# A cross-attention block on one Trainium2 core: where the attention weights are turned, and the order of pairs 3 to 5 and of the end

## The chip, the cores and the metric

The kernel runs on 1 core of one Trainium2 chip. The metric is the device time in microseconds (us). Five engines work side by side, each through its own instructions in their written order: TensorE (PE in the profile: matmuls; PEld: the weight loads that go with them), VectorE (DVE), ScalarE (ACT), GpSimd (POOL) and SyncE (SP, which here only issues DMAs). ACT's queue issues DMAs too.

## The reference

All tensors are float32. There are 128 sequences of 128 tokens with 256 features, `x` for the queries and `ctx_1024` for keys and values; 16 heads of 16 features.

```python
q = (query @ Wq + bq).reshape(b, s, 16, 16).transpose(0, 2, 1, 3)      # k and v likewise, from ctx
scores = einsum('bhqd,bhkd->bhqk', q, k) / sqrt(16)
scores = where(j < i, scores, -1e30)                                     # strictly earlier keys alone
attn = softmax(scores); attn[:, :, 0, :] = 0
ctx = einsum('bhqk,bhkd->bhqd', attn, v)
x = layer_norm(query + ctx @ Wo + bo, ln1_g, ln1_b)
out = layer_norm(x + relu(x @ W1 + b1) @ W2 + b2, ln2_g, ln2_b)         # W1: 256x1024, W2: 1024x256
```

## The kernel before, in words

**Tiling.** Two sequences make a pair; there are 64 pairs, p = 0 to 63, and 256 tokens in each. Scores have queries in partitions: the upper half of the queries (`hi` = 1, against all 128 keys) and the lower half (`hi` = 0, against the first 64 keys) are apart, since the mask leaves out later keys. The upper half has 2048 elements in a partition and is worked in two parts (`ONE`, heads 0 to 7, and `TWO`, heads 8 to 15), the lower half has 1024 (`ALL`).

**The stages of a pair**, with the lines that the profile names:
- `tokens` (L243, DVE) turns the loaded blocks of x or ctx into `xT`, `cT`; `load`, `load_tokens` and `load_ahead` (L92, L99) issue their DMAs on SP.
- `queries`, `keys` (L257, PE; L268 and L279, ACT) and `values` (L289, PE), with `values_out` (L299, L304 on ACT, and the DMA `vd<-vz`, L303, on ACT's queue).
- `scores` (L323) or `scores_both` (L357) on PE. `scores` makes one half, in PSUM banks 0 to 3. `scores_both` makes both: the upper half in banks 0 to 3, the lower half in banks 6, 7, 4 and 5.
- `mask` (L371, DVE) adds the mask and so empties the banks into `sm`; `maximum` (L382 on DVE, and on POOL the subtraction, L383); `exponential` (L390, ACT); `sums` (L402 and L403 on DVE, and on POOL the multiplication by the inverse of the sum, L404).
- `turn` (L417, DVE): a transposition of the weights in blocks of 32x32, into `tb`; three for a pair (upper `ONE`, upper `TWO`, lower). `bring` (L432): 16 DMAs, u = 0 to 15, that carry block row i = u // 4 and block column j = u % 4 of `tb` to its place in `pT`. `tb` and `pT` have one buffer each, so the `bring` of a pair starts after the `weigh` of the pair before.
- `weigh` (L464, L474, PE): weights times values, 96 short matmuls into bank 7. It reads blocks i = 0 and 1 (u = 0 to 7) for the first sequence of the pair (s = 0), then i = 2 and 3 (u = 8 to 15) for the second (s = 1). `context` (L486, ACT) copies the result to `cxT`.
- `attention_out` (L493, PE, bank 5), `attention_sum` (L519, DVE), `stats` (L506, L507, DVE), `deviation` and `shift` (L513, L514, L558, POOL), `norm1` (L535, ACT), `residual1` (L547, L550, POOL), `add_bo` (L250, POOL).
- `turn_x1`: a transposition `tbx` on DVE (L644), then `across`: four DMAs `x1t<-tbx` to DRAM (L235) and, when they have landed, one DMA `x1T<-x1t` back (L238).
- `hidden` (L680, PE; L686, ACT): x1 times W1 for eight chunks f, in four steps of two chunks that use banks 2, 3, 4 and 0, each followed by two ReLUs into `hT`. `second` (L698, PE, bank 6): eight matmuls in the program for each sequence s. The profile has twice as many matmuls as the program, here as everywhere, each with its weight load.
- `second_sum` (L706, DVE), `stats`, `scale_and_shift` (POOL), `norm2` (L572, ACT), `finish` (L578, L579, POOL), `store` (L587, the DMA `out_dram<-t` on ACT's queue).

**What sets the order.** `manual_schedule` keeps each engine's instructions in the order in which the program writes them; waits between engines are added by the framework from what reads and writes what. A bank that gets a new tile waits for the last reader of the old one. The start (pairs 0 and 1, before the functions below) and the functions `third` (L859, p = 2), `fourth` (L910, p = 3) and, for p = 4 to 63, `step(p)` (L937) write the order by hand; the lines after the loop (L1002 to L1078) empty the pipeline.

In `step(p)` PE has: `weigh(p-2)`, `scores_both(p)`, `queries(p+1)`, `attention_out(p-2)`, `keys(p+1)`, `values(p)`, `hidden(p-3)`, `second(p-3)`. DVE has the three `turn(p-1, ...)` between the masks and maxima of pair p. SP has: the loads of `load_ahead(p)`, then `bring(p-1)`, after the third turn, then the five DMAs of `turn_x1(p-2)`. In the last step and after the loop half of the weights, u = 8 to 15, are brought on ACT's queue.

In `fourth` the scores of pair 3 are made by `scores_both`, and `second(0)`, which writes bank 6, stands after them; the low scores of strip 0, in bank 6 too, are emptied by `mask(3, 0, A)`, the last masks of the pair.

Of the kernel before, what the change touches and what calls it, by code (L numbers as in the profile page):

```python
# [10 lines left out]
ALU = mybir.AluOpType  # L11
# [8 lines left out]
def tile_cross_attention_block(  # L20
# [205 lines left out]
                )  # L226
        return pt

    def across(dst, src, name):


        n = src.shape[2]
        mid = dram.tile([NS, NS, 32, n], F32, tag=name[: name.index("_")], name=name)
        for i in range(NS):
            nc.sync.dma_start(  # L235
                mid[i].rearrange("j b n -> b j n"), src[32 * i : 32 * i + 32]
            )
        nc.sync.dma_start(dst, mid.rearrange("i j b n -> (j b) i n"))  # L238

    def tokens(p, which):  # L240
        st = states.setdefault(p, {})
        st[which + "T"] = proj.tile([P, KC, TP], F32, tag=which + "T", name=f"{which}T_{p}")
        nc.vector.transpose(  # L243
            st[which + "T"], blocks_of.pop((which, p)).rearrange("p k u f -> p k (u f)")
        )
# [17 lines left out]
    def queries(p):  # L263
        st = states[p]
        st["qT"] = proj.tile([P, KC, TP], F32, tag="qT", name=f"qT_{p}")
        pq = project(wq, st["xT"], at_bank(4, f"pq_{p}") if p > 3 else bank(f"pq_{p}"))
        for m in range(KC):
            nc.scalar.activation(  # L268
                st["qT"][:, m, :], pq[:, m * TP : (m + 1) * TP], AF.Identity,
                bias=bqs_c[:, m : m + 1], scale=QSCALE,  # L270
            )
# [116 lines left out]
    def exponential(p, hi, part):  # L388
        sm = states[p]["sm", hi]
        nc.scalar.activation(sm[:, part, :], sm[:, part, :], AF.Exp)  # L390
# [229 lines left out]
    def scale_w1():  # L620
        for k in range(KC):
            nc.scalar.activation(
                w1[:, k, :], w1[:, k, :], AF.Identity, bias=0.0, scale=g1_c[:, k : k + 1]
            )
# [13 lines left out]

    def turn_x1(p):
        st = states[p]
        tb = ffn.tile([P, NS, 4 * 32], F32, tag="tbx", name=f"tbx_{p}")
        nc.vector.transpose(  # L644
            tb.rearrange("p j (u a) -> p u j a", a=32),
            st["x1"].rearrange("p s (k j a) -> p (s k) j a", k=KC, a=32),
        )
        x1T = ffn.tile([P, NS, 4 * 32], F32, tag="x1T", name=f"x1T_{p}")
        across(x1T, tb, f"x1t_{p}")
        st["x1T"] = x1T.rearrange("p i (s k a) -> p s i k a", s=2, k=KC)  # L650

    def turn_x1_on_pe(p):
# [37 lines left out]
            if between:  # L690
                between(f)

    def second(p, s, fs=range(FC)):
        st = states[p]
        if s == 0 and fs[0] == 0:
            st["py"] = at_bank(6, f"py_{p}")
        for f in fs:
            nc.tensor.matmul(  # L698
                st["py"][:, s * D : (s + 1) * D], st["hT"][:, f, s * P : (s + 1) * P],
                w2[:, f, :], start=(f == 0), stop=(f == FC - 1),  # L700
            )

    def second_sum(p):
        st = states[p]
# [137 lines left out]
    def load_ahead(p):  # L842
        if p % 2 == 0 and p + 4 < NP:
            load([p + 4, p + 5], "x")
        if p % 2 == 1:
            if p + 3 < NP:
                load([p + 3, p + 4], "c")
            if 3 < p < NP - 1:
                load_tokens((p + 1) // 2)
# [9 lines left out]
    def third():  # L859
# [47 lines left out]
        residual1(p - 1)  # L907
        hidden(0, range(3 * FC // 4, FC), lambda f: bring(p, nc.scalar, EVERY[8:]))

    def fourth():  # L910
        p = 3
        load_ahead(p)
        scores_both(p)
        mask(p, 0, B)
        mask(p, 1, A)
        maximum(p, 1, ONE)
        second(0, 0)
        exponential(p, 1, ONE)
        mask(p, 1, B)
        maximum(p, 1, TWO)  # L920
        second(0, 1)
        scale_w1()
        mask(p, 0, A)
        maximum(p, 0, ALL)
        queries(p + 1)
        exponential(p, 1, TWO)
        nc.gpsimd.tensor_tensor(b1e_c, b1e_c, b1_c, ALU.add)
        sums(p, 1, ONE)
        exponential(p, 0, ALL)
        tokens(p + 2, "x")  # L930
        keys(p + 1)
        second_sum(0)
        sums(p, 1, TWO)
        sums(p, 0, ALL)
        tokens(p + 2, "c")

    def step(p):  # L937
        last = p == NP - 1
        load_ahead(p)
        weigh(p - 2)  # L940
        context(p - 2)
        scores_both(p)
        if p > 4:
            second_sum(p - 4)
        turn(p - 1, 1, 0)
        if p > 4:
            residual1(p - 3)
            finish(p - 5)
            add_bo(p - 1)
        mask(p, 0, B)  # L950
        mask(p, 1, A)
        maximum(p, 1, ONE)
        turn(p - 1, 1, 1)
        if not last:
            queries(p + 1)
        if p > 4:
            store(p - 5)
        attention_out(p - 2)
        mask(p, 1, B)
        maximum(p, 1, TWO)  # L960
        exponential(p, 1, ONE)
        turn(p - 1, 0, 0)
        bring(p - 1, nc.sync, EVERY[: 8 if last else 16])
        mask(p, 0, A)
        maximum(p, 0, ALL)
        if not last:
            keys(p + 1)
        else:
            bring(p - 1, nc.scalar, EVERY[8:])
        exponential(p, 1, TWO)  # L970
        attention_sum(p - 2)
        values(p)
        stats(p - 4, states[p - 4]["t2"], 2)
        stats(p - 2, states[p - 2]["t1"], 1)
        scale_and_shift(p - 4)
        deviation(p - 2, 1)
        shift(p - 2, 1)
        values_out(p)
        sums(p, 1, ONE)
        exponential(p, 0, ALL)  # L980
        sums(p, 1, TWO)

        def between(f):
            if f == 4:
                norm1(p - 2)

        hidden(p - 3, range(FC), between)
        norm2(p - 4)
        sums(p, 0, ALL)
        if p + 2 < NP:  # L990
            tokens(p + 2, "x")
            tokens(p + 2, "c")
        turn_x1(p - 2)
        second(p - 3, 0)
        second(p - 3, 1)

    third()
    fourth()
    for p in range(4, NP):
        step(p)  # L1000

    p = NP - 1  # L1002
    weigh(p - 1)
    context(p - 1)
    second_sum(p - 3)
    turn(p, 1, 0)
    turn(p, 1, 1)
    turn(p, 0, 0)
    bring(p, nc.sync, EVERY[:8])
    residual1(p - 2)  # L1010
    finish(p - 4)
    add_bo(p)
    attention_out(p - 1)
    attention_sum(p - 1)
    attention_stats(p - 1)
    shift(p - 1, 1)
    stats(p - 3, states[p - 3]["t2"], 2)
    scale_and_shift(p - 3)
    bring(p, nc.scalar, EVERY[8:12])
    store(p - 4)  # L1020
    hidden(p - 2, range(FC // 2))
    bring(p, nc.scalar, EVERY[12:])
    hidden(p - 2, range(FC // 2, FC))
    norm1(p - 1)
    turn_x1(p - 1)
    norm2(p - 3)
    second(p - 2, 0)
    second(p - 2, 1)
# [3 lines left out]
    second_sum(p - 2)  # L1032
    residual1(p - 1)
    finish(p - 3)
    attention_out(p)
    attention_sum(p)
    attention_stats(p)
# [1 line left out]
    stats(p - 2, states[p - 2]["t2"], 2)  # L1039
    scale_and_shift(p - 2)  # L1040
    store(p - 3)
    norm1(p)
    turn_x1(p)
    hidden(p - 1, range(FC))
    norm2(p - 2)
    residual1(p)
    finish(p - 2)
# [66 lines left out]
```

## Time and profile before

| | us |
|---|---|
| median of 3 runs | 1601.88 |
| lowest and highest of them | 1599.53 and 1605.21 |
| the profiled execution's own time | 1603.7 |
| span of the profiled execution, first to last instruction | 1601.9 |
| PE busy in it | 1565.4 |
| POOL busy, DVE busy, ACT busy | 1304.0, 1272.8, 794.6 |
| first matmul of weigh(4), of step 6 | 137.5 |
| first matmul of weigh(61), of step 63 | 1515.9 |
| last matmul ends | 1596.5 |

How to read it: all durations come from one profiled execution. The profile calls the weight loads PEld and lists them apart from the matmuls that they serve. "issue" is time in which an engine waited for nothing that the profile shows. Matmuls overlap: a float32 matmul of 256 columns is listed with 379 to 382 ns, and the next one starts 216 ns after it. "PEclk" is the clock granted to TensorE, 1.00 being full speed. The queue q8 of kind "instruction" carries the program itself.

### The profile page before, as it was taken

Reading aid. Unit: us, or ns where it says so; the run is one execution under the profiler, and the core shown is the slowest. Engines: PE = TensorE matmul, PEld = TensorE weight load, DVE = VectorE, ACT = ScalarE, POOL = GpSimd, SP = SyncE. Lnnn points to the kernel's source line nnn. Section 1 sums busy time; section 2 is a strip of 40 time slices with the busy share of each in tenths; the row PEclk is TensorE's granted clock in tenths of the full one; section 3 lists DMA queues with packets and bytes.
Section 4 is the critical chain, followed back from the end, with each engine's and each line's share of the span. In section 5 each row is a group of like instructions: output and inputs, shape, how many; then the busy total and the mean of one; then the engine's idle time right before and its main releaser. Section 6 shows DMA issues by size and latency. Waiting matters only on the chain.

```text
span 1601.9 us, 41519 instructions
## 1 busy us (share of the span) xinstructions
PE 1565.4 (98%) x16486; PEld 1355.3 (85%) x16486; DVE 1272.8 (79%) x2125; ACT 794.6 (50%) x1616; POOL 1304.0 (81%) x1229
## 2 busy tenths in 40 slices
PE   8799999999999999999999999999999999999988
PEld 7678888888888888888888888888888888888867
DVE  7878878878878778778788888878778788788752
ACT  5545445445445455455455455455454454454432
POOL 6868888888887787888888888888888878888863
PEclk9899999999999999999999999999999999999999
DMA  9436566656665556666556666656566555664441
GB/s 198 104 75 143 132 145 146 136 131 143 135 143 127 128 137 139 140 139 137 132 139 142 140 139 140 142 129 138 134 143 136 128 135 135 145 141 112 116 104 53
DMA packets 481808, 212.22 MB, mean 132 GB/s; under 512 B 349008, under 2 KB 449616, under 8 KB 481616
## 3 DMA queue, kind: packets, MB, share of 16 engines
q1 hardware_dynamic: 395248, 182.03, 50.8%
q10 hardware_dynamic: 86368, 27.54, 7.0%
q8 instruction: 131, 2.15, 0.6%
q14 instruction: 61, 0.50, 0.1%
HBM read 70.26 MB, written 33.29 MB: 65 GB/s over the span
## 4 chain that ended last, share of the span: by engine, by line
PE 87%; DVE 4%; DMA 3%; SPq 2%; issue 1%; POOL 1%; ACT 1%; ACTq 0%; POOLq 0%; DVEq 0%
PE py L698 25%; PE ph L680 24%; PE pq L257 7%; PE po L493 6%; PE pk L257 6%; PE pv L289 6%; PE pss L357 6%; PE pc L474 3%; PE pc L464 2%; SPq L432 2%; DVE sm L371 2%; DMA vd<-vz 1%; DVE nmx L382 1%; DVE tb L417 1%; POOL sm L383 1%
## 5 line engine op out<-in xcount | busy, mean ns | idle before, releaser
L383 POOL TENSOR_TENSOR sm<-sm,nmx 128x1024 f32<-128x1024 f32 x192 | 364.2, 1897 | 203.9 <-DVE nmx L382 200.1
L698 PE MATMUL py<-w,hT 128*128 128x256 f32 x2016 | 451.3, 382 | 14.3 <-DVE sm L371 8.0
L680 PE MATMUL ph<-x1T,w 128*128 128x256 f32 x2048 | 453.3, 379 | 0.5 <-DVE sm L371 0.5
L698 PEld LDWEIGHTS py<-w,hT 128*128 128x128 f32 x2016 | 386.9, 192 | 68.6 <-DVE sm L371 8.2
L680 PEld LDWEIGHTS ph<-x1T,w 128*128 128x128 f32 x2048 | 388.7, 190 | 54.4 <-DVE sm L371 0.9
L404 POOL TENSOR_TENSOR sm<-sm,rs 128x1024 f32<-128x1024 f32 x192 | 359.2, 1898 | 11.8 <-DVE rs L403 11.7
L390 ACT ACTIVATE sm<-sm 128x1024 f32<-128x1024 f32 x192 | 202.8, 1057 | 164.8 <-POOL sm L383 156.6
L371 DVE TENSOR_TENSOR sm<-pss,neg 128x512 f32<-128x512 f32 (+1 forms) x512 | 250.6, 539 | 23.9 <-PE pss L357 20.3
L382 DVE TENSOR_REDUCE nmx<-sm 128x8 f32<-128x1024 f32 (+1 forms) x192 | 234.2, 1220 | 6.6
L706 DVE TENSOR_TENSOR t<-py,x1b 128x512 f32<-128x512 f32 x63 | 43.6, 692 | 240.2 <-issue 180.4
L402 DVE TENSOR_REDUCE su<-sm 128x8 f32<-128x1024 f32 (+1 forms) x192 | 225.7, 1175 | 7.9 <-ACT sm L390 7.9
L417 DVE STREAM_TRANSPOSE tb<-sm 128x1024 f32<-128x1024 f32 x186 | 229.2, 1234 | 1.7 <-DMA x1t<-tbx 1.4
L486 ACT COPY cxT<-pc 128x508 f32<-128x508 f32 x64 | 37.3, 583 | 347.0 <-PE pc L474 347.0
L686 ACT ACTIVATE hT<-ph,b1e_c 128x256 f32<-128x256 f32 x504 | 195.4, 471 | 17.4 <-PE ph L680 17.3
L268 ACT ACTIVATE qT<-pq,bqs_c 128x256 f32<-128x256 f32 x126 | 52.8, 470 | 190.2 <-PE pq L257 190.2
L279 ACT ACTIVATE kT<-pk,bkh,half 128x256 f32<-128x256 f32 x252 | 121.6, 563 | 11.9 <-PE pk L257 11.7
L257 PE MATMUL pq<-xT,wq 128*128 128x256 f32 x504 | 126.5, 394 | 0.5 <-DVE sm L371 0.5
L493 PE MATMUL po<-wo,cxT 128*128 128x256 f32 x512 | 122.1, 382 | 1.5 <-ACT cxT L486 1.5
L289 PE MATMUL pv<-wv,cT 128*128 128x256 f32 x512 | 120.9, 379 | 0.0
L257 PE MATMUL pk<-cT,wk 128*128 128x256 f32 x504 | 119.2, 379 | 0.0
L493 PEld LDWEIGHTS po<-wo,cxT 128*128 128x128 f32 x512 | 97.6, 191 | 15.7 <-ACT cxT L486 2.1
L357 PE MATMUL pss<-kT,qT 32*64 32x256 f32 (+1 forms) x3904 | 103.3, 330 | 6.5 <-issue 5.3
(100 smaller groups left out, 1849.5 us busy)
## 6 DMA issues: line engine op xcount, KB each, us to landing
pT<-tb SPq DMA_DIRECT2D x968, 96.0 KB, 2.2
x1t<-tbx SPq DMA_DIRECT2D x252, 64.0 KB, 1.8
x1T<-x1t SPq DMA_DIRECT2D x63, 256.0 KB, 3.9
out_dram<-t ACTq DMA_DIRECT2D x63, 256.0 KB, 3.2
xb<-in_x_dram SPq DMA_DIRECT2D x124, 128.0 KB, 4.0
cb<-in_ctx_dram SPq DMA_DIRECT2D x124, 128.0 KB, 4.5
x<-in_x_dram SPq DMA_DIRECT2D x31, 512.0 KB, 5.5
vd<-vz ACTq DMA_DIRECT2D x64, 128.0 KB, 3.3
```

What stands on the lines that cost most here:

```text
L257: nc.tensor.matmul(ps[:, m * TP : (m + 1) * TP], w[:, k, m * P : (m + 1) * P], src[:, k, :], start=(k == 0), stop=(k == KC - 1),)
L289: nc.tensor.matmul(pv[:, s * D : (s + 1) * D], st["cT"][:, k, s * P : (s + 1) * P], wv[:, k, :], start=(k == 0), stop=(k == KC - 1),)
L371: nc.vector.tensor_tensor(st["sm", hi][:, 4 * r : 4 * r + 4, :], st["sps", hi][r][:, : 4 * n].rearrange("p (n j) -> p n j", j=n), no[:, No ...
L382: nc.vector.tensor_reduce(nmx[:, part], sm[:, part, :], AX.X, ALU.max, negate=True)
L383: nc.gpsimd.tensor_tensor(sm[:, part, :], sm[:, part, :], nmx[:, part, None].to_broadcast([P, part.stop - part.start, n]), ALU.add,)
L390: nc.scalar.activation(sm[:, part, :], sm[:, part, :], AF.Exp)
L402: nc.vector.tensor_reduce(su, sm[:, part, :], AX.X, ALU.add)
L404: nc.gpsimd.tensor_tensor(sm[:, part, :], sm[:, part, :], rs[:, :, None].to_broadcast([P, part.stop - part.start, n]), ALU.mult,)
L417: nc.vector.transpose(st["tb"][:, :, at : at + 256].rearrange("p j (n a) -> p n j a", a=32), st["sm", hi].rearrange("p h j -> p (h j)")[:, ...
L493: nc.tensor.matmul(po[:, s * D : (s + 1) * D], cxT[:, k, s, :], wo[:, k, :], start=(k == 0), stop=(k == KC - 1),)
L680: nc.tensor.matmul(ph[:, i * TP : (i + 1) * TP].rearrange("p (s i a) -> p s i a", s=2, a=32), w1[:, k, (f + i) * P : (f + i + 1) * P], st[ ...
L698: nc.tensor.matmul(st["py"][:, s * D : (s + 1) * D], st["hT"][:, f, s * P : (s + 1) * P], w2[:, f, :], start=(f == 0), stop=(f == FC - 1),)
```

## The change

- **Turns.** `step(p)` no longer turns the weights of pair p-1 between the masks of pair p. It turns those of pair p itself at its own end, after `tokens`: upper `ONE`, then `turn_x1(p-2)`, then upper `TWO` and lower.
- **Brings.** All 16 DMAs of `bring(p-1)` are issued on SP, right after the scores of step p, ahead of `load_ahead(p)`, in the order u = 8 to 15, then 0 to 7 (`LATE_FIRST`). That holds for the last step and after the loop too, where half of them were on ACT's queue.
- **Pairs 3 to 5.** `fourth` makes the scores of pair 3 in two halves (`scores`), with `second(0)` after the first half and `weigh(2)`, `context(2)` ahead of the second half; it takes over the turns and the bring of pair 3, `attention_out(2)` with what follows it, `turn_x1(2)` and `hidden(1)`. A new function `fifth` (p = 4) has `values(4)`, `second(1)`, the turns of pair 4 and half of `hidden(2)`. `step` starts at p = 5, and its first call has the other half of `hidden(2)`.
- **End.** After the loop the first two chunks of `hidden` of each of the pairs 61 and 62 stand ahead of `attention_out`, and `norm1` of the next pair stands within the other six. `across` and `turn_x1` take the queue as an argument, and the x1 of pair 62 goes over ACT's queue.
- **Empty instructions.** `second` takes `pad`; in the steps p = 28 and p = 51 each of its 16 matmuls of the program is followed by 7 `nop`s on TensorE.

```diff
@@ -226,16 +226,16 @@
                 )
         return pt
-    def across(dst, src, name):
+    def across(dst, src, name, queue):
         n = src.shape[2]
         mid = dram.tile([NS, NS, 32, n], F32, tag=name[: name.index("_")], name=name)
         for i in range(NS):
-            nc.sync.dma_start(
+            queue.dma_start(
                 mid[i].rearrange("j b n -> b j n"), src[32 * i : 32 * i + 32]
             )
-        nc.sync.dma_start(dst, mid.rearrange("i j b n -> (j b) i n"))
+        queue.dma_start(dst, mid.rearrange("i j b n -> (j b) i n"))
     def tokens(p, which):
         st = states.setdefault(p, {})
@@ -638,7 +638,7 @@
-    def turn_x1(p):
+    def turn_x1(p, queue=nc.sync):
         st = states[p]
         tb = ffn.tile([P, NS, 4 * 32], F32, tag="tbx", name=f"tbx_{p}")
         nc.vector.transpose(
@@ -646,7 +646,7 @@
             st["x1"].rearrange("p s (k j a) -> p (s k) j a", k=KC, a=32),
         )
         x1T = ffn.tile([P, NS, 4 * 32], F32, tag="x1T", name=f"x1T_{p}")
-        across(x1T, tb, f"x1t_{p}")
+        across(x1T, tb, f"x1t_{p}", queue)
         st["x1T"] = x1T.rearrange("p i (s k a) -> p s i k a", s=2, k=KC)
     def turn_x1_on_pe(p):
@@ -690,7 +690,7 @@
             if between:
                 between(f)
-    def second(p, s, fs=range(FC)):
+    def second(p, s, fs=range(FC), pad=0):
         st = states[p]
         if s == 0 and fs[0] == 0:
             st["py"] = at_bank(6, f"py_{p}")
@@ -699,6 +699,8 @@
                 st["py"][:, s * D : (s + 1) * D], st["hT"][:, f, s * P : (s + 1) * P],
                 w2[:, f, :], start=(f == 0), stop=(f == FC - 1),
             )
+            for _ in range(pad):
+                nc.tensor.nop(hint="pad", nofuse=True)
     def second_sum(p):
         st = states[p]
@@ -907,66 +909,107 @@
         residual1(p - 1)
         hidden(0, range(3 * FC // 4, FC), lambda f: bring(p, nc.scalar, EVERY[8:]))
+    LATE_FIRST = (*EVERY[8:], *EVERY[:8])
+
     def fourth():
         p = 3
+        load_ahead(p)
+        scores(p, 1)
+        mask(p, 1, A)
+        maximum(p, 1, ONE)
+        second(0, 0)
+        mask(p, 1, B)
+        maximum(p, 1, TWO)
+        exponential(p, 1, ONE)
+        second(0, 1)
+        tokens(p + 2, "c")
+        sums(p, 1, ONE)
+        exponential(p, 1, TWO)
+        second_sum(0)
+        sums(p, 1, TWO)
+        weigh(p - 1)
+        context(p - 1)
+        scores(p, 0)
+        scale_w1()
+        nc.gpsimd.tensor_tensor(b1e_c, b1e_c, b1_c, ALU.add)
+        queries(p + 1)
+        mask(p, 0, A)
+        mask(p, 0, B)
+        maximum(p, 0, ALL)
+        exponential(p, 0, ALL)
+        turn(p, 1, 0)
+        turn(p, 1, 1)
+        attention_out(p - 1)
+        attention_sum(p - 1)
+        sums(p, 0, ALL)
+        attention_stats(p - 1)
+        shift(p - 1, 1)
+        tokens(p + 2, "x")
+        keys(p + 1)
+        turn(p, 0, 0)
+        bring(p, nc.sync, LATE_FIRST)
+        stats(0, states[0]["t2"], 2)
+        scale_and_shift(0)
+        norm1(p - 1)
+        turn_x1(p - 1)
+        hidden(1, range(FC))
+        norm2(0)
+
+    def fifth():
+        p = 4
         load_ahead(p)
         scores_both(p)
         mask(p, 0, B)
         mask(p, 1, A)
         maximum(p, 1, ONE)
-        second(0, 0)
-        exponential(p, 1, ONE)
+        queries(p + 1)
         mask(p, 1, B)
         maximum(p, 1, TWO)
-        second(0, 1)
-        scale_w1()
+        exponential(p, 1, ONE)
         mask(p, 0, A)
         maximum(p, 0, ALL)
-        queries(p + 1)
+        keys(p + 1)
         exponential(p, 1, TWO)
-        nc.gpsimd.tensor_tensor(b1e_c, b1e_c, b1_c, ALU.add)
+        values(p)
+        values_out(p)
         sums(p, 1, ONE)
         exponential(p, 0, ALL)
-        tokens(p + 2, "x")
-        keys(p + 1)
-        second_sum(0)
         sums(p, 1, TWO)
         sums(p, 0, ALL)
+        tokens(p + 2, "x")
         tokens(p + 2, "c")
+        second(1, 0)
+        second(1, 1)
+        turn(p, 1, 0)
+        turn(p, 1, 1)
+        turn(p, 0, 0)
+        hidden(2, range(FC // 2))
     def step(p):
         last = p == NP - 1
-        load_ahead(p)
         weigh(p - 2)
         context(p - 2)
         scores_both(p)
-        if p > 4:
-            second_sum(p - 4)
-        turn(p - 1, 1, 0)
-        if p > 4:
-            residual1(p - 3)
-            finish(p - 5)
-            add_bo(p - 1)
+        bring(p - 1, nc.sync, LATE_FIRST)
+        load_ahead(p)
+        second_sum(p - 4)
+        residual1(p - 3)
+        finish(p - 5)
+        add_bo(p - 1)
         mask(p, 0, B)
         mask(p, 1, A)
         maximum(p, 1, ONE)
-        turn(p - 1, 1, 1)
         if not last:
             queries(p + 1)
-        if p > 4:
-            store(p - 5)
+        store(p - 5)
         attention_out(p - 2)
         mask(p, 1, B)
         maximum(p, 1, TWO)
         exponential(p, 1, ONE)
-        turn(p - 1, 0, 0)
-        bring(p - 1, nc.sync, EVERY[: 8 if last else 16])
         mask(p, 0, A)
         maximum(p, 0, ALL)
         if not last:
             keys(p + 1)
-        else:
-            bring(p - 1, nc.scalar, EVERY[8:])
         exponential(p, 1, TWO)
         attention_sum(p - 2)
         values(p)
@@ -984,45 +1027,44 @@
             if f == 4:
                 norm1(p - 2)
-        hidden(p - 3, range(FC), between)
+        hidden(p - 3, range(FC // 2 if p == 5 else 0, FC), between)
         norm2(p - 4)
         sums(p, 0, ALL)
         if p + 2 < NP:
             tokens(p + 2, "x")
             tokens(p + 2, "c")
+        turn(p, 1, 0)
         turn_x1(p - 2)
-        second(p - 3, 0)
-        second(p - 3, 1)
+        turn(p, 1, 1)
+        turn(p, 0, 0)
+        pad = 7 if p in (28, 51) else 0
+        second(p - 3, 0, pad=pad)
+        second(p - 3, 1, pad=pad)
     third()
     fourth()
-    for p in range(4, NP):
+    fifth()
+    for p in range(5, NP):
         step(p)
     p = NP - 1
     weigh(p - 1)
     context(p - 1)
+    bring(p, nc.sync, LATE_FIRST)
     second_sum(p - 3)
-    turn(p, 1, 0)
-    turn(p, 1, 1)
-    turn(p, 0, 0)
-    bring(p, nc.sync, EVERY[:8])
     residual1(p - 2)
     finish(p - 4)
     add_bo(p)
+    hidden(p - 2, range(2))
     attention_out(p - 1)
     attention_sum(p - 1)
     attention_stats(p - 1)
     shift(p - 1, 1)
     stats(p - 3, states[p - 3]["t2"], 2)
     scale_and_shift(p - 3)
-    bring(p, nc.scalar, EVERY[8:12])
     store(p - 4)
-    hidden(p - 2, range(FC // 2))
-    bring(p, nc.scalar, EVERY[12:])
-    hidden(p - 2, range(FC // 2, FC))
-    norm1(p - 1)
-    turn_x1(p - 1)
+    hidden(p - 2, range(2, FC), lambda f: norm1(p - 1) if f == 4 else None)
+    turn_x1(p - 1, nc.scalar)
     norm2(p - 3)
     second(p - 2, 0)
     second(p - 2, 1)
@@ -1032,6 +1074,7 @@
     second_sum(p - 2)
     residual1(p - 1)
     finish(p - 3)
+    hidden(p - 1, range(2))
     attention_out(p)
     attention_sum(p)
     attention_stats(p)
@@ -1039,9 +1082,8 @@
     stats(p - 2, states[p - 2]["t2"], 2)
     scale_and_shift(p - 2)
     store(p - 3)
-    norm1(p)
+    hidden(p - 1, range(2, FC), lambda f: norm1(p) if f == 4 else None)
     turn_x1(p)
-    hidden(p - 1, range(FC))
     norm2(p - 2)
     residual1(p)
     finish(p - 2)
```

## The prediction, before the result was known

> **What bounds the kernel now.** I read the page first: engine shares, the queue of instructions, the chain.
>
> ```profile
> span 1601.9 us, 41519 instructions
> PE 1565.4 (98%) x16486; PEld 1355.3 (85%) x16486; DVE 1272.8 (79%) x2125; ACT 794.6 (50%) x1616; POOL 1304.0 (81%) x1229
> ...
> q8 instruction: 131, 2.15, 0.6%
> ...
> PE 87%; DVE 4%; DMA 3%; SPq 2%; issue 1%; POOL 1%; ACT 1%; ACTq 0%; POOLq 0%; DVEq 0%
> ```
>
> TensorE is busy for all but 36.5 us, so an edit can gain only where TensorE stands still or runs at a lower clock. Second, the waits of TensorE in three windows (opening, steps, end): what it waited for, us in total, times, longest.
>
> ```profile
> PE py L698 <- DVE sm L371: 8.0, 1, 8.0
> ...
> PE pc L464 <- DMA pT<-tb: 1.8, 1, 1.8
> ```
> ```profile
> PE pss L357 <- issue: 5.3, 6, 1.4
> PE pc L464 <- DMA x1t<-tbx: 0.3, 1, 0.3
> PE pc L464 <- DMA pT<-tb: 0.2, 1, 0.2
> ```
> ```profile
> PE py L698 <- ACT hT L686: 6.3, 1, 6.3
> PE po L493 <- ACT cxT L486: 1.5, 2, 0.8
> PE ph L680 <- DVE sm L371: 0.5, 1, 0.5
> ```
>
> The opening waits once for a mask, the end once for a ReLU; between them no engine holds TensorE, only "issue" does. Third, stretches of time (us, then PE, PEld, DVE, ACT, POOL busy, granted clock, DMA).
>
> ```profile
> 62.00:72.00 10.00, 2.03 (x67) 1.55 (x65) 9.90 (x15) 1.91 (x4) 9.13 (x8) 0.79 0.76 192
> 72.00:78.00 6.00, 6.00 (x14) 4.83 (x15) 3.37 (x5) 2.34 (x3) 5.47 (x4) 0.50 0.63 111
> ...
> 887.50:911.40 23.90, 23.90 (x257) 20.90 (x256) 19.85 (x33) 12.28 (x25) 20.33 (x20) 1.00 0.63 145
> ```
> ```profile
> 24.00:26.80 2.80, 0.20 (x2) 0.00 (x0) 2.77 (x5) 2.07 (x6) 2.80 (x3) 0.99 1.04 354
> 26.80:30.20 3.40, 3.35 (x16) 3.28 (x16) 2.46 (x4) 1.69 (x3) 3.27 (x2) 0.50 1.32 236
> ...
> 504.60:508.00 3.40, 3.40 (x10) 2.66 (x9) 3.37 (x5) 1.23 (x3) 1.71 (x2) 0.50 0.89 216
> ```
>
> A clean step is 23.94 us from one weigh to the next, and TensorE is full in it. An idle stretch is paid twice: after the 8 us one the clock was 0.50 until 78; after one of 2.65 us (up to 26.86), and after one of 1.41 us (up to 503.30), it was 0.50 for 3.4 us, a loss of 1.7 us. Last, the timeline of an "issue" wait:
>
> ```profile
> 474.96 1.57 PE L357 MATMUL pss<-kT,qT 32*64 32x128 f32 x60
> 477.57 0.43 PE L357 MATMUL pss<-kT,qT 32*64 32x128 f32 x4 [1.04 <-issue]
> ```
>
> Of 64 score matmuls, 60 ran, then nothing was there to run. The q8 row (packets, MB, share) explains it: 2.15 MB over the trace's 32,972 matmuls and weight loads and 640 semaphore waits on TensorE is 64 B each, so a packet holds 256 instructions. A step issues 522 (256 matmuls, 256 weight loads, 10 waits), two packets. Weigh and scores are 320 of them in 3.1 us. In the trace's DMA records a packet starts at 475.1 and takes 1.0 us; the stall ends at 477.57. It began 312 instructions into the step, so that block began at 56. Its beginning moves 10 back per step (522 = 2 x 256 + 10). Stalled steps are 20, 21, 24 and 45 to 54 (not all of them): beginnings of 62 down to -28.
>
> **The change part by part.**
>
> *Turns and brings.* Three DVE turns (1.16 each from start to start) go from between the masks to the end of the step that made the weights. POOL's last multiply (L404) sets the last turn. In step 911.5 the masks move up: the third maximum ends at 921.3 instead of 923.5, POOL's third add at 923.3 instead of 925.6, its small operations (3.3) at 926.6, three multiplies (5.6) at 932.3; the last turn then ends near 933.6, and DVE's next work (L706) comes at 935.6. 2 us are left, so the step stays at TensorE's 23.94. The 16 issues on SP (0.63 each, 10 us) now run from about 1.6 us into the step and land by 14, ten microseconds before weigh asks for them; loads, 4.2 to 5.3 us of issues, wait behind them, but serve a later step; the four x1t issues and x1T (0.38, after a landing of 1.35) come after both: 19 us of 23.94. The waits on pT and x1t vanish: about 2 us over the run. In the middle the move itself gains no more.
>
> *Waits and nops.* Weigh has 8 EVENT_SEMAPHOREs per step (L464, x488). The new order brings the second half of the weights (s=1) first, so the wait for s=0, which weigh makes first, covers s=1: four fewer, an estimate from the code. Then a step is 518 and the block moves 6 back per step. From 56 in step 20, with four saved in 15 to 23 steps, it stands near 68 at step 28 and would reach 62 at step 29. There 112 nops (7 x 16) put it to -50, past the band; 23 steps later (256 - 112 = 144, 6 each) it stands near 74, and the second padded step, 51, skips again. So the band is never entered, give or take a step. From 137.46 (weigh of pair 4) to 1515.94 (pair 61) are 57 steps: 1378.5 less 57 x 23.94 is **13.9 us of excess**: 11.3 in steps with "issue" waits (their half clock within), 2 of pT and x1t, the rest small. I leave 1 us.
>
> No NOP is in the trace. Nearest row: EVENT_SEMAPHOREs on TensorE, 51 ns each, 106 apart; four of them between 883.57 and 883.98 left the matmuls at their 216 ns. Seven at 51 are 0.36 per `second` matmul pair, under its 0.43 (hidden); at 106 they are 0.74, 16 x 0.31 = 5.0 over, less the 3.9 us by which the sequencer runs ahead (weigh's waits pass at 883.6, weigh starts at 887.5): 1.1, with the empty queue up to 2 us a step. Bounds 0 (an empty instruction gains nothing itself) to 4 for both; if nothing hid them, 224 x 0.051 to 0.106 = 11.4 to 23.7. I take 1, by the undisturbed matmuls. Middle: 13.9 - 1 - 1 = **11.9**.
>
> [...]
>
> *Pairs 3 to 5.* `second(0)` no longer needs the bank of the low scores; it starts at 63.2 instead of 71.97 and ends at 70.1. I laid the new order out by row durations. TensorE: weigh(2) waits for pT (last issue ends 69.0 + 2.2 = 71.3; idle 1.3), low scores to 73.4, three products (1.75 each) to 78.7, hidden(1) 6.9 to 85.6. The other chain: masks and maxima from 65.97 to 70.7, second exponential 73.9, its sums 75.3, low masks and maximum 77.9, add 79.8, exponential 80.9, sums 82.2, multiply 84.2, deviation and shift 85.9, norm1(2) on ACT 87.0, six ReLUs behind it 89.2. So scores_both(4), which needs their banks, starts at 89.3: **a new idle of 3.7 + 0.5**. Then 7 us of scores and products, second(1) to 103.5; x1T(2), on SP behind the 16 brings (85.5 to 95.3), lands near 103, just in time. Idle now 8.0+0.5+0.5+0.5+1.8+0.4 = 11.7, and 3.0 of half clock: 14.7. After: 1.3+3.7+0.5+0.3 = 5.8, and 1.7 for the clock: 7.5. Gain **7.2** (bounds 3, if x1T is late by the 3.9 us of another landing, to 9.5).
>
> *End.* Weights no longer go over ACT's queue, where eight issues (6.43) held the exponential, ReLUs and TensorE 6.34 us. Idle now 0.5+6.3+0.7+0.8 = 8.3, half clock 3.0: 11.3. After, hidden(61) comes right after weigh(62), 22.8 us after weigh(61); x1T(61) leaves DVE at 18.5, +2.0 issues, +1.4, +2.8 to 4.1 = near 25.3: idle 2.5. x1T(63) is late by 0.7, ReLUs by 0.3: 3.5, with 1.7 for the clock 5.2. x1T(62), on ACT's queue, is in time. Gain **6.0** (3 to 8). The 5.4 us behind the last matmul stay.
>
> [...]
>
> Sum: 7.2 + 11.9 + 6.0 = 25.1. Span 1601.9 - 25.1 = 1576.8; the profiled execution's own 1603.7 gives 1578.6. It stands 1.8 above the median 1601.88, so the median is predicted at **1577**.
>
> **The rivals.**
> 1. *The block does not skip the band* (no waits saved, or the padded steps fall elsewhere): some 9 of the 11.3 stay. For it: the saved waits are not in this trace. Against: the distance of 23 steps fits 144/6. 1577 + 9 = **1586**.
> 2. *Nops are not hidden*: 11.4 to 23.7 less the 1 taken: **1587 to 1600**. Against: 883.57.
> 3. *Slower: ACT waits for a bring.* Brings wait for a transfer that they do not use (SP's waits list `vd<-vz` 47.8 us, 52 times): DMAs share semaphores. If ACT's store (5 us into a step) gets that of the twelfth bring (lands near 11), ACT stops for some 3.7 us beyond its need, ahead of the exponential. ReLU output leads `second` by 1.5 us (903.0 against 904.48), so 2.2 us a step, 58 steps: 128, **near 1705**; slower from 0.43 us a step, a delay of 1.9. Against: stores so far are issued at once, four brings or more would have to be ordered ahead of their time.
>
> **How the numbers follow.** Forecast 0.67, rival 1 0.18, rival 2 0.06, rival 3 and its like 0.09. The summed bounds are 31.4 (9.5 + 13.9 + 8) and 9 (3 + 3 + 3, the middle with 4 of nops and 7 of stalls): 1570 to 1593. I say 1569 to 1591. A measurement tells about 0.3% (5 us) from no change: faster 0.87 (forecast, rival 1, most of 2), same 0.04, slower 0.09.
>
> **What would show it.** Right: second(0) near 63 and no 8 us wait; a wait of scores_both(4) for ReLUs near 89; half as many L464 waits; steps at 23.94 in 28 and 51 too; "issue" waits gone; hidden(61) waiting for x1T. Wrong: idle before weigh in the padded steps, "issue" waits elsewhere, or ACT waiting ahead of `out_dram`.

## The result, and the profile after

| | before | after |
|---|---|---|
| median, us | 1600.7 | 1625.64 |
| lowest and highest | 1599.24 and 1605.21 | 1622.66 and 1627.3 |
| span of the profiled execution | 1601.9 | 1623.0 |
| its own time | 1603.7 | 1624.7 |

The ratio is 1.0149, with a 95% interval from 1.0122 to 1.0176. **The change made the kernel slower; 1577 was predicted, and the time lies outside the range.**

The page after, with the lines that answer to the first ones of before: the span, the engines' busy times, and the chain of work that ended last, by engine and by line.

```profile
span 1623.0 us, 41609 instructions
...
PE 1588.8 (98%) x16486; PEld 1359.0 (84%) x16486; DVE 1266.6 (78%) x2125; ACT 787.8 (49%) x1616; POOL 1304.0 (80%) x1229
...
DVE 31%; DMA 16%; SPq 14%; PE 13%; ACT 13%; POOL 9%; issue 4%; DVEq 0%; ACTq 0%; POOLq 0%
SPq L432 14%; DVE tb L417 12%; DMA vd<-vz 9%; DVE sm L371 7%; DMA pT<-tb 6%; ACT sm L390 6%; POOL sm L383 6%; DVE nmx L382 5%; ACT kT L279 4%; PE ph L680 4%; PE py L698 3%; POOL sm L404 2%; DVE tbx L644 2%; DVE t L708 2%; DVE su L402 2%
```

TensorE is still called busy for 98%, with the same 16486 matmuls, but its busy time grew by 23.4 us, and its share of the chain fell from 87% to 13%. In its place stand SP at the brings (L432), VectorE at the turns (L417) and two transfers. So here the busy share does not say who bounds the kernel; the chain does.

**Where the time came from.** Three parts, each between two marks, from the matmuls' starts:

| | before | after | difference | forecast |
|---|---|---|---|---|
| weigh(0) to weigh(4) | 106.5 (31.0 to 137.5) | 105.3 (31.4 to 136.6) | -1.2 | -7.2 |
| weigh(4) to weigh(61), 57 steps | 1378.5 | 1407.6 | +29.1 | -11.9 |
| weigh(61) to the last matmul's end | 80.6 | 73.3 | -7.3 | -6.0 |

The stretch ahead of weigh(0) is 0.4 longer, what follows the last matmul is as long as before (5.45); the sum is the span's +21.0. The loss lies in the middle, where a step takes 24.69 us on the mean in place of 24.18 before and of 23.94 for a clean one. TensorE's time went into one line of a step, the 64 score matmuls (busy us, mean ns | idle before, releaser; before, after, and the wait of their weight loads after: us, times, longest; after, 64 matmuls of pair 3 stand on another line, L323):

```profile
L357 PE MATMUL pss<-kT,qT 32*64 32x256 f32 (+1 forms) x3904 | 103.3, 330 | 6.5 <-issue 5.3
```
```profile
L357 PE MATMUL pss<-kT,qT 32*64 32x256 f32 (+1 forms) x3840 | 129.0, 335 | 15.3 <-DVE t L708 10.6
```
```profile
PEld pss L357 <- DVE t L708: 32.0, 52, 2.1
```

They wait for `t` of L708: `second_sum`, which empties bank 6, and bank 6 takes the last scores. On VectorE's timeline of one step (start, duration, instructions) it stands behind the turns:

```profile
902.17 1.25 DVE L417 STREAM_TRANSPOSE tb<-sm 128x1024 f32<-128x1024 f32 x1 [4.52 <-POOL x1b L547]
903.34 0.67 DVE L644 STREAM_TRANSPOSE tbx<-x 128x512 f32<-128x512 f32 x1
903.94 2.33 DVE L417 STREAM_TRANSPOSE tb<-sm 128x1024 f32<-128x1024 f32 x2
906.19 0.65 DVE L708 TENSOR_TENSOR t<-py,x1b 128x512 f32<-128x512 f32 x1
...
926.96 1.25 DVE L417 STREAM_TRANSPOSE tb<-sm 128x1024 f32<-128x1024 f32 x1 [4.71 <-DMA pT<-tb]
```

VectorE stands still for 4.5 us ahead of the first turn. The releaser at 902.17 is named as POOL, but the last bring landed at 901.86, and at 926.96 (last landing at 926.88) the profile names the brings: those of pair p-1 must have read `tb` before turn(p, 1, 0) may write it, for there is one `tb`. SP's timeline in the same step:

```profile
904.04 1.78 SPq L235 DMA_DIRECT2D x1t<-tbx  x4
908.50 0.38 SPq L238 DMA_DIRECT2D x1T<-x1t  x1
909.04 16.19 SPq L432 DMA_DIRECT2D pT<-tb  x16
```

The 16 brings, 0.63 us apart when nothing holds them (10.1 us in all), take 16.2. The single issues with the semaphore each raises (from the trace) say why:

```
issue     queue  DMA                semaphore  lands
909.04    SP     bring, first        101       911.89
909.61    ACT    store               102       912.45
912.47    SP     bring, second       102       915.85
...
916.29    SP     bring, seventh      108       918.63
916.42    ACT    vd                  100       919.40
919.42    SP     bring, eighth       100       921.53
...
924.63    SP     bring, last         100       926.88
```

Eight semaphores (100 to 105, 107 and 108) go round among all the DMAs of both queues, in an order that is not the one of issue (vd raises 100, ahead of the first bring's 101, and is issued after the seventh), and an issue waits until the DMA that had its semaphore last has landed (in these rows it starts 0.02 us later: 912.47 after 912.45, 919.42 after 919.40). The second bring waits for the store, which ACT issued 0.57 us after the first; the eighth waits for vd. So a loop closes: turn, x1t, its landing, x1T, brings with two stops, last landing, turn. From 902.17 to 926.96 it takes 24.8 us, more than TensorE's 23.94. SP's waits over the run, for x1t's landing and for the two DMAs of ACT's queue (us, times, longest):

```profile
SPq L238 <- DMA x1t<-tbx: 175.2, 81, 5.1
SPq L432 <- DMA vd<-vz: 164.0, 56, 5.3
SPq L432 <- DMA out_dram<-t: 96.4, 42, 4.8
```

Before, the stops for vd were there too (47.8 us, 52 times), but the turns did not wait for the brings: all the idle time of VectorE ahead of its 186 turns came to 1.7 us.

### The profile page after: what moved, and what is told of

The parts are those of the page before. It is cut to its first block, busy times and chain, and to the rows that moved or that the text cites. A ratio compares the mean times of both kernels' runs of the same rounds, so it can differ in the third digit from the quotient of the medians.

```text
span 1623.0 us, 41609 instructions
## 1 busy us (share of the span) xinstructions
PE 1588.8 (98%) x16486; PEld 1359.0 (84%) x16486; DVE 1266.6 (78%) x2125; ACT 787.8 (49%) x1616; POOL 1304.0 (80%) x1229
## 4 chain that ended last, share of the span: by engine, by line
DVE 31%; DMA 16%; SPq 14%; PE 13%; ACT 13%; POOL 9%; issue 4%; DVEq 0%; ACTq 0%; POOLq 0%
SPq L432 14%; DVE tb L417 12%; DMA vd<-vz 9%; DVE sm L371 7%; DMA pT<-tb 6%; ACT sm L390 6%; POOL sm L383 6%; DVE nmx L382 5%; ACT kT L279 4%; PE ph L680 4%; PE py L698 3%; POOL sm L404 2%; DVE tbx L644 2%; DVE t L708 2%; DVE su L402 2%
## 5 line engine op out<-in xcount | busy, mean ns | idle before, releaser
L698 PE MATMUL py<-w,hT 128*128 128x256 f32 x2016 | 446.1, 379 | 0.8 <-ACT hT L686 0.8
L698 PEld LDWEIGHTS py<-w,hT 128*128 128x128 f32 x2016 | 382.7, 190 | 54.3 <-ACT hT L686 2.4
L417 DVE STREAM_TRANSPOSE tb<-sm 128x1024 f32<-128x1024 f32 x186 | 221.9, 1217 | 258.9 <-DMA pT<-tb 142.6
L686 ACT ACTIVATE hT<-ph,b1e_c 128x256 f32<-128x256 f32 x504 | 202.4, 466 | 36.0 <-PE ph L680 33.0
L357 PE MATMUL pss<-kT,qT 32*64 32x256 f32 (+1 forms) x3840 | 129.0, 335 | 15.3 <-DVE t L708 10.6
L357 PEld LDWEIGHTS pss<-kT,qT 32*64 32x64 f32 x3840 | 89.3, 132 | 46.1 <-DVE t L708 32.0
L257 PEld LDWEIGHTS pq<-xT,wq 128*128 128x128 f32 x504 | 91.7, 192 | 20.8 <-issue 10.1
```

What stands on the lines that cost most here:

```text
L257: nc.tensor.matmul(ps[:, m * TP : (m + 1) * TP], w[:, k, m * P : (m + 1) * P], src[:, k, :], start=(k == 0), stop=(k == KC - 1),)
L357: nc.tensor.matmul(st["sps", hi][r][s * HP : (s + 1) * HP, m * 2 * n : (m + 1) * 2 * n].rearrange("p (e j) -> p e j", e=2), st["qT"][strip ...
L417: nc.vector.transpose(st["tb"][:, :, at : at + 256].rearrange("p j (n a) -> p n j a", a=32), st["sm", hi].rearrange("p h j -> p (h j)")[:, ...
L698: nc.tensor.matmul(st["py"][:, s * D : (s + 1) * D], st["hT"][:, f, s * P : (s + 1) * P], w2[:, f, :], start=(f == 0), stop=(f == FC - 1),)
```

## The experiments

**Theory**: the loop just told makes the step; shorten it below TensorE's 23.94, and the step is 23.94. **Rivals**: POOL's multiplications or TensorE's empty instructions made the steps long; or the new opening and end are worth nothing.

**1. `tb` with two buffers.**

```diff
-        st["tb"] = soft.tile([P, NS, (H + HH) * 32], F32, tag="tb", name=f"tb_{p}")
+        st["tb"] = soft.tile([P, NS, (H + HH) * 32], F32, tag="tb", name=f"tb_{p}", bufs=2)
```

> The changed kernel with two buffers for tb, so that a turn need not wait until the last bring of the pair before has read it. Theory 1 (a closed loop on SP: turn waits for the last bring to land, the brings wait for landings of ACT's store and vd, the next bring waits for the turn): the step falls from 24.7 to 23.94 us, 57 steps give back about 43 us, some 1582 us (1576 to 1590), and the wait of TensorE's scores for second_sum (L708) goes. Theory 2 (the moved turns wait for POOL's last multiplies, POOL's chain is what has become late): a second tb changes nothing, 1620 to 1630 us.

1598.45 us (0.9979 of before, 0.9965 to 0.9993), 27 less than the change. That lies between the two theories. The wait of the turns is gone, but the stops of the brings stay (148.8 us for vd, 76.8 for the store), and x1T, which follows on SP, is late for hidden up to 1.1 us in single steps. Weigh(4) to weigh(61) takes 1378.3, as before the change, and 13.3 more than in experiment 2. So the turn's wait is part of the loop, but without it alone the steps are not clean. That SP's queue with its stops is then itself too long for a step is how these waits read; no run tests it apart.

**2. Store and vd behind the brings on SP**, `tb` single. All DMAs of a step then stand in one queue.

```diff
-        nc.scalar.dma_start(
+        (nc.sync if 0 <= p <= NP - 6 else nc.scalar).dma_start(
             out[2 * p : 2 * p + 2].rearrange("b p d -> p b d"), states.pop(p)["t2"]
-        nc.scalar.dma_start(st["vd"][HP:], st["vz"][:HP, :, :, 2:4, :])
+        (nc.sync if p > 4 else nc.scalar).dma_start(st["vd"][HP:], st["vz"][:HP, :, :, 2:4, :])
```

> The changed kernel with tb as it is (one buffer), but the store and the vd transfer of steps 5 and later are issued on SP, behind the brings and the loads, so that no bring waits for a transfer of another queue. Theory 1: the 16 brings take 10 us instead of some 16 to 18, the last lands 14 us into the step, the turns start when POOL is done, the step is 23.94 us: about 1583 us (1577 to 1595; SP has two more issues). If the loop is not made long by those landings but by tb's one buffer alone, or by POOL (theory 2): 1620 to 1630 us.

1583.37 us (0.9881 of before, 0.9866 to 0.9896). The middle takes 1364.9, which is 57 steps of 23.95. SP has time to spare now: in the middle its brings wait for weigh to leave `pT`, and for no transfer.

```profile
SPq L432 <- PE pc L474: 111.0, 58, 6.3
```

TensorE waits for nothing in the whole stretch. The brings run from 1.6 us into the step and the last lands 14.6 us into it (medians of 50 steps; 6.1 and 22.8 in the changed kernel), so the turns never wait for `tb`, though there is still one. This settles the cause of the loss: the loop over ACT's two DMAs, and not POOL, and not the empty instructions, which this kernel has.

**3. One of the two alone on SP.** In the first kernel only the store moves, in the second only vd (pairs 5 to 63).

> The changed kernel with the store alone (out_dram, pairs 0 to 58) issued on SP; vd stays on ACT's queue, tb stays single. Theory of the loop (turn, x1t, bring, turn), which had 4.6 us a step of stops of the brings, 2.9 for vd and 1.7 for the store, and a slack below TensorE's 23.94 of 1.9 without both: with the vd stop alone the loop is 23.0 to 24.9, so steps of 23.94 to 24.4 and 1583 to 1605. Rival (a stop spared at one place is taken at the next, since every DMA waits for the one eight earlier): 1615 to 1625.

1584.03 us (0.9892; 0.9875 to 0.9909), steps of 23.94 but for three of 24.15 to 24.32.

> The changed kernel with vd alone (pairs 5 to 63) issued on SP; the store stays on ACT's queue, tb stays single. Theory of the loop (any stop of the brings counts once the loop is longer than TensorE's step; with the store moved alone 1584 us, the loop then had 0.5 to 1.9 us to spare): the stop for the store of 1.7 us a step alone fits too: steps of 23.94 to 24.2, 1582 to 1598. Rival (it is the store alone that holds the loop, since it stops the second bring and so nearly the whole train): steps of 24.4 or more, 1608 or more.

1588.32 us (0.9903; 0.9888 to 0.9918), all steps at 23.94 but four: two that waited for "issue" (the steps 50 and 52, 5.1 us more) and two of 24.13 and 24.37. SP's stops, first of the kernel with the store moved, then of that with vd moved:

```profile
SPq L432 <- DMA vd<-vz: 140.7, 57, 3.8
```
```profile
SPq L432 <- DMA out_dram<-t: 171.1, 53, 6.1
```

A stop of 2.5 us a step stays in the one, of 3.0 in the other, and neither shows in the step. (Why the steps 50 and 52 of the second kernel wait for "issue", although it has the empty instructions, stays open.) The rival, that a stop spared at one place comes back in full at the next, is out for the first and half right for the second: the store's stop grew from 96.4 to 171.1. The store alone doesn't hold the loop either, as the second expectation's rival had it. Both stops together are needed for the loss: a loop costs nothing until it is longer than TensorE's step, and this one was 0.8 us longer.

**4. The change's opening and end, with the turns and brings where they were before**, and no empty instructions.

```diff
+        load_ahead(p)
...
-        bring(p - 1, nc.sync, LATE_FIRST)
-        load_ahead(p)
         second_sum(p - 4)
+        turn(p - 1, 1, 0)
...
         maximum(p, 1, ONE)
+        turn(p - 1, 1, 1)
...
         exponential(p, 1, ONE)
+        turn(p - 1, 0, 0)
+        bring(p - 1, nc.sync, EVERY)
...
-        turn(p, 1, 0)
         turn_x1(p - 2)
-        turn(p, 1, 1)
-        turn(p, 0, 0)
...
```

> The opening (pairs 3 to 5) and the order of the end of the changed kernel, but the turns and brings of the steps where the kernel before has them (all 16 on SP), and no empty instructions. Theory 1 (the whole loss lies in the moved turns and brings): the opening gives 1 us and the end some 7, as they did in the changed kernel's profile: 1590 to 1595 us. Rival (opening or end are at fault too): 1601 us or more.

1603.2 us (1.0009; 0.9996 to 1.0023). As the rival said, nothing was gained. But the graft brings waits of its own (ReLUs held TensorE for 2.1 us at 133.65, x1T for 3.5 and 2.1 near the end), so it doesn't price the change's opening and end; the marks of experiment 2 do: 1.2 us in the opening, 4.0 at the end.

**5. The empty instructions.** First `tb` with two buffers and no empty instructions, then experiment 2 without them, then the kernel before with nothing but empty instructions added, in four steps chosen by its own drift of 10 a step.

```diff
-        pad = 7 if p in (28, 51) else 0
+        pad = 0
```
```diff
+        pad = 7 if p in (19, 33, 47, 61) else 0
-        second(p - 3, 0)
-        second(p - 3, 1)
+        second(p - 3, 0, pad=pad)
+        second(p - 3, 1, pad=pad)
```

> As the kernel with two tb, without the empty instructions of steps 28 and 51. If instruction blocks that begin within weigh starve the scores (6 back per step, the band of 62 to -28 from step 29 to about 43), issue waits come back in those steps: 4 to 12 us more than with the empty instructions. If the empty instructions do nothing but cost time: the same within 2 us, or faster.

1608.01 us (1.0046; 1.0027 to 1.0064), 9.6 more than with them. "issue" waits come back between the steps 28 and 41, where the expectation had the packet's beginning in the band, from 29 to about 43:

```profile
PE pss L357 <- issue: 5.2, 7, 2.4
PE pq L257 <- issue: 1.9, 2, 1.6
```

> The run with store and vd on SP, without the empty instructions. Theory of the program's packets: 518 instructions a step, so from about step 28 to 41 the weigh and score matmuls cross a packet's beginning and stall, where now no step is over 24.1: 9 to 12 us slower, 1592 to 1596, all of it in those steps. Rival (the stalls come from the late transfers, which this kernel does not have): 1582 to 1585 with every step at 23.94.

1587.83 us (0.9912; 0.9896 to 0.9929): 4.5 more, less than expected. Behind step 6 the longer steps are 28 to 33 alone (24.1 to 24.88, together 3.3 over). TensorE's timeline in step 31 shows the form known from before, a stop 59 matmuls into the 64 scores:

```profile
736.51 1.57 PE L357 MATMUL pss<-kT,qT 32*64 32x128 f32 x59
738.63 0.44 PE L357 MATMUL pss<-kT,qT 32*64 32x128 f32 x5 [0.55 <-issue]
```

> The kernel before, with nothing changed but 7 empty instructions behind each matmul of second in the steps 19, 33, 47 and 61. Theory of the packets: a packet's beginning moves 10 instructions back each step, stalls fall in the steps where it lies between 62 and -28, and 112 instructions more jump over that band each time (14 steps later it is back at 60 to 64): the 11.3 us of the stalled steps go, 1588 to 1593, and no TensorE wait for issue is left in the steps 20 to 24 and 45 to 54. Rival (the stalls have another cause, or the empty instructions cost what they save): 1599 to 1604.

1594.54 us (0.9958; 0.9942 to 0.9973): 6.7 less than before, from empty instructions alone, a little short of the expected. The waits of the scores for "issue" are gone, and the steps 20 to 24 and 45 to 54 take 23.94, apart from those at the padded ones and step 50 (24.71); the middle falls from 1378.5 to 1370.4. Part of the cost had not been expected: `second` keeps its 7.07 us in a padded step, but that step is 0.73 to 0.76 longer and the next one 0.33 to 0.51. So the waits of the kernel before depend on the place of the packets: moved as forecast, they are gone. The account is not complete: why the steps 34 to 41 did not stall in the second kernel stays open, as do the two stalls of experiment 3.

**6. The opening mended.** Experiment 2 with vd of pair 4 on SP too, and norm1(2) and turn_x1(2) behind hidden(1). (Shown is the edit against the changed kernel, without that of the store.)

```diff
-        nc.scalar.dma_start(st["vd"][HP:], st["vz"][:HP, :, :, 2:4, :])
+        (nc.sync if p > 3 else nc.scalar).dma_start(st["vd"][HP:], st["vz"][:HP, :, :, 2:4, :])
-        norm1(p - 1)
-        turn_x1(p - 1)
         hidden(1, range(FC))
+        norm1(p - 1)
+        turn_x1(p - 1)
```

> As the run with store and vd on SP, but vd of pair 4 on SP too, and in the opening norm1(2) and turn_x1(2) behind hidden(1). Theory of the queues (in the opening the same two things cost: the ReLUs of hidden(1) stand behind norm1(2) on ACT, 3.8 us of TensorE idle; and the fourth x1t issue of pair 2 waits from 98.5 to 105.05 on SP for the landing of vd(4), which ACT issued at 102.25, so x1T(2) lands 2.5 us late): idle of 3.8 falls below 1.2, the 2.5 goes, and with them 6.8 + 3.4 us at half clock, worth 5.1: 1571 to 1577, weigh(4) at 126 to 130 instead of 136.3. Rival (VectorE's chain of pair 4 bounds the opening, so that an earlier scores_both only waits later): 1580 to 1584, weigh(4) at 134 or later.

1577.47 us (0.9847; 0.9828 to 0.9865). The wait of 3.8 us for ReLUs fell to 0.55; but x1T(2) still came 3.3 us late, at 104.97, since its first issue stood behind the 16 brings of pair 3 until 98.4. Weigh(4) starts at 131.4 (136.3 in experiment 2; 126 to 130 expected): some half of what was expected.

**7. The end mended, and then the rest of the opening.** The first kernel is experiment 6 with `attention_out(62)` ahead of the first two chunks of hidden(61) again, and in the last step the turn of x1 ahead of those of the weights. The second also sends x1 of pair 2, in `fourth`, over ACT's queue, past the brings.

```diff
-    hidden(p - 2, range(2))
     attention_out(p - 1)
+    hidden(p - 2, range(2))
...
+        if last:
+            turn_x1(p - 2)
         turn(p, 1, 0)
-        turn_x1(p - 2)
+        if not last:
+            turn_x1(p - 2)
```
```diff
-        turn_x1(p - 1)
+        turn_x1(p - 1, nc.scalar)
```

> The run with the opening mended, and at the end attention_out(62) ahead of the first two chunks of hidden(61) again, and in the last step the turn of x1 ahead of the turns of the weights. Theory of the end (TensorE waits 3.45 us for x1T(61) at 1523.0, and 3.4 us at half clock follow, 1.7 more; attention_out fills 1.7 of it and x1T comes 1.3 to 1.9 earlier): idle 0.8 or less, no half clock, 4 to 5 us less: 1572 to 1574. Rival (attention_out waits as long for cxT as hidden did for x1T): 1576 to 1578.

1574.98 us (0.9823; 0.9809 to 0.9836). From weigh(61) to the last matmul's end it takes 72.1 us, and 74.7 in experiment 6: the wait of 3.5 for x1T(61) became one of 0.8 for `cxT`, but one of 1.5 ahead of weigh(63) is new. 2.5 us less on the medians, between theory and rival.

> The run before this one in this list, and in the opening x1 of pair 2 goes over ACT's queue, past the 16 brings of pair 3 on SP. Theory (TensorE waits 3.27 us at 105.0 for x1T(2), which lands 104.97 because its first issue stands behind the brings until 98.4, and 3.4 us at half clock follow): x1T(2) lands near 95, both go, 4.5 to 5 us less: 1567 to 1569, weigh(4) near 126.5 instead of 131.4. Rival (the brings of pair 3 or VectorE bound it, or ACT's waits for landings hold the products' outputs): 1571 to 1574.

**1571.56 us (0.9801 of before; 0.9788 to 0.9814)**, the fastest of all. The expected 1567 to 1569 was missed by 3 us, and the time is one that the rival had named; but TensorE's wait for x1T(2) is gone, and weigh(4) starts at 126.6 as foretold: the kernel it builds on came out 1 to 3 us above its own expectation, and had weigh(4) at 129.2 already, since there the 2.7 us of waiting for x1T(2) were not followed by half clock (mean granted clock 0.999). Its page:

```profile
span 1569.6 us, 41730 instructions
...
PE 1553.9 (99%) x16486; PEld 1348.6 (86%) x16486; DVE 1277.7 (81%) x2125; ACT 781.4 (50%) x1616; POOL 1305.7 (83%) x1229
```

Compare its PE line with that of after: 34.9 us less busy time for the same 16486 matmuls.

## Why the prediction was wrong

**The step that failed** is the one on turns and brings: "2 us are left, so the step stays at TensorE's 23.94. The 16 issues on SP (0.63 each, 10 us) now run from about 1.6 us into the step and land by 14, ten microseconds before weigh asks for them". In the step shown they ran from 5.2 us into it (909.04, weigh at 903.82) and landed by 23.1 (926.88). Two things were left out.
- *The wait that the change adds.* turn(p) at the end of a step must wait until the brings of p-1 have read `tb`. Nothing about it stands in the prediction; it went through the queues that the moved work passes, but not through the buffers that it writes. In order behind this wait stands `second_sum`, behind that bank 6, behind that the scores. Alone it would have cost nothing: in experiment 2, with the same one `tb`, the last bring lands by 14.6, and the turns don't wait for it.
- *The stops.* The prediction counted SP's issues end to end, although it had itself read that brings wait for transfers that they don't use. Rival 3 used that fact, but for ACT only, where a wait for a bring would hold the exponential. It was the other way round: the brings waited for ACT's transfers. With 16.2 us for the brings in place of 10, and x1T waiting up to 5 us for a landing amid the loads, the "19 us of 23.94" became a loop of 24.8.

The middle: +29.1 in place of -11.9. With the loop broken (experiment 2) it is -13.5: of the excess of 13.9 only 0.4 is left, and the 2 us put down for residue and empty instructions were hardly needed.

**The opening**, 7.2 forecast, 1.2 found, below its lower bound of 3. The order of events was right: second(0) no longer waits, weigh(2) waits 0.9 (1.3 said), scores_both(4) waits 3.7 us for ReLUs at 90.24 (3.7 at 89.3 said). Two sizes were off, as the waits after show:

```profile
PE pss L357 <- ACT hT L686: 3.9, 2, 3.7
...
PE ph L680 <- DMA x1T<-x1t: 2.4, 1, 2.4
```

x1T(2), "just in time" in the prediction, is 2.4 late, and that too is a stop by a shared semaphore: the fourth x1t issue waits from 98.9 to 105.49 for vd(4), which ACT issued at 102.69. The lower bound had this case (3, if x1T is late). And half clock held for 6.8 and 3.4 us (at 90.48 and 110.96), a loss of 5.1, where 1.7 was put down.

**The end**, 6.0 forecast, 7.3 found: hidden(61) waits 3.0 for x1T (2.5 said), and the half clock that was priced at 1.7 did not come. In experiment 2 it came, for 6.8 us (mean granted clock 0.992, and 0.994 in after), and the end gained 4.0; that this part came out near its forecast is luck in part (see the last section). Two sums of the prediction are a little off: 11.3 less 5.2 is 6.1, and 0.87 for "faster" holds a third of rival 2's 0.06, not most of it.

**Right**: the L464 EVENT_SEMAPHOREs are 249 (488 before; half said), and a step has 518 instructions on TensorE (522 before), as said; no score matmul of the changed kernel waits for "issue"; the empty instructions, 13 ns each and in the median 71 ns apart (224 of them in the trace of after), leave `second` at 7.07 us. The runs of experiment 5 show that they are worth 4.5 to 9.6 us. With the loop broken by moving the two DMAs (experiment 2), the change gives 1583, inside the range.

## What to carry to other kernels

When work moves to an earlier place, list what its **output buffer** is still read by, not only the inputs and the queues: a single buffer turns a chain into a loop, and a loop is priced by its full period against the bound engine's step, with every wait in it. Where DMAs of several queues share semaphores, as here, the queue with a long train of issues paid for the landing of each transfer that another queue slipped in (stops of 2.5 to 2.9 us in the step shown); put behind the train in the same queue, they cost an issue each (0.44 and 0.66 us in experiment 2), and the stops were gone. A loop that was only 0.8 us too long cost 43 us in 57 steps. Either of the two stops taken away was enough to end that; the second buffer gave back 27 us.

## What the runs showed of the hardware that was not expected

**In these traces the clock fell by windows, not by gaps.** The prediction took an idle stretch of 1.41 or 2.65 us as enough for half clock. After the change one of 2.97 us cost nothing. In the traces of before and after every stretch of one granted clock but the last is a multiple of 3.413 us (at half clock 3.413, 6.827 and 10.240 us, at full clock 13.653 to 1505.278), so time is cut on that grid here. These are stretches of after, then of experiment 6 (length, then PE, PEld, DVE, ACT, POOL busy, granted clock, DMA):

```profile
1565.04:1568.45 3.41, 2.37 (x101) 1.82 (x99) 1.82 (x2) 0.58 (x1) 3.33 (x4) 1.00 0.31 76
1568.45:1571.87 3.42, 1.49 (x7) 1.37 (x8) 0.00 (x0) 0.00 (x0) 2.89 (x3) 1.00 0.77 211
1571.87:1575.28 3.41, 3.41 (x18) 3.00 (x17) 1.12 (x2) 0.84 (x2) 0.00 (x0) 1.00 0.61 171
```
```profile
102.85:106.26 3.41, 1.25 (x6) 1.12 (x7) 3.11 (x4) 0.00 (x0) 3.33 (x4) 1.00 1.04 183
106.26:109.68 3.42, 3.42 (x10) 2.68 (x9) 0.00 (x0) 0.84 (x2) 3.34 (x3) 0.50 0.91 85
```

The gap of 2.97 us fell across a border, 1.0 and 1.9 us idle in two windows, and both successors ran at full clock; in the other kernel 2.2 us fell into one window, and the next ran at 0.50. On the grids of before and after, from the first weigh to the last matmul, the windows at full clock that were followed by half clock had 3.41, 1.41 and 3.41 us of idle TensorE in before (from 64.31, 501.22 and 1532.04) and 3.17 and 2.42 in after (from 87.07 and 107.55). Of those followed by full clock, the most idle had 1.53 and 1.66 in before (from 112.10 and 1528.63) and 1.93 in after (the second row). So between 1.41 and 1.93 lie both kinds; what decides there, no run shows. The length of a gap alone did not set its price: 2.97 us across a border cost nothing, and 1.41 us inside a window 1.7 (3.4 us at half clock). The grid lies differently in each of these three traces (borders at 504.63, 1568.45 and 106.26, which no multiple of 3.413 joins).
